# Renumbered expert rows, a combine tile from TensorE, and head outputs stored by halves

## The chip, the core and the metric

The kernel runs on one core of a Trainium2 chip. A core has five engines with queues of their own: TensorE (matrix products, PE in the profile, with PEld for the loading of its weights), VectorE (DVE), ScalarE (ACT), GpSimd (POOL) and SyncE (SP), which only issues transfers here. Sixteen DMA engines move data between the chip's memory (HBM, "DRAM" in the code) and the on-chip SBUF; TensorE writes to PSUM. The metric is the device time in microseconds of one execution. Before the change it was 1862.59 us, the median of three runs (1858.78 to 1864.37).

## What is computed

One transformer block over 2048 tokens of width 256: attention with 16 heads of 128 whose weights come as codes and scales, then a mixture of 8 experts with inner width 176, of which each token uses two. A layernorm stands before and after each half.

```python
x = x + _layernorm(attn(_layernorm(x)))        # 16 heads, softmax over 2048 keys
x = x + _layernorm(ffn(_layernorm(x)))
# ffn:
router_logits = jnp.einsum('bsh,he->bse', x, Wr)
probs = jax.nn.softmax(router_logits.astype(jnp.float32), axis=-1)
topk_w, topk_idx = jax.lax.top_k(probs, K)                       # K = 2
topk_w = topk_w / jnp.sum(topk_w, axis=-1, keepdims=True)
combine = jnp.einsum('bsk,bske->bse', topk_w, one_hot(topk_idx, E))
g = jnp.einsum('bsh,ehi->besi', x, Wg)
u = jnp.einsum('bsh,ehi->besi', x, Wu)
y = jnp.einsum('besi,eih->besh', jax.nn.silu(g) * u, Wd)
out = jnp.einsum('bse,besh->bsh', combine, y)
```

The kernel computes all experts for all tokens and multiplies the inner activations of each expert by the token's combine weight, which is zero for six experts of eight. So the experts become one dense layer with EI = 8×176 = 1408 inner rows, in 11 chunks of 128 (NCH).

## The kernel before

**Attention.** A loop runs over 256 steps, 16 heads times 16 tiles of 128 query rows. In each step TensorE makes a tile's scores against 2048 keys (L484 to L488), VectorE their maximum (L489), ScalarE the exponentials (L500). The probabilities are split into two float16 parts, `ph` (ScalarE, L514) and `pl` (VectorE, L529), and each part is transposed by a DMA that SP issues (L517, L535) into `pth` and `ptl`, 512 KB each. TensorE then multiplies them by the values (`pv_part`, L552), 13 half-steps behind. The finished output of a head for a block of 512 tokens is split into a high and a low half in float16 (`o`, GpSimd, L567 and L568) and stored to DRAM in `ot_d[b]`, laid out [128, head, 2, 512], by a DMA that GpSimd issues (L569).

**Hand-over.** From the last head on (`late`, L700), other loads share SP's queue with the transposes: output-projection weights, the gate weights `gu_raw` for `gw`, and the head outputs `oi` (`load_oi`, L681: four heads, both parts, 256 of the 512 tokens; 32 such loads in all). `op_mm` (L802) projects them (64 matmuls for half a block) and VectorE takes the layernorm statistics. The lines L1068 to L1138 write this stretch out by hand, in the order in which each engine gets its instructions. There the weights `wg`, `wu` and `wd` are split into two float32r parts by `split_piece` (L655): a copy on ScalarE and a subtraction on GpSimd. The stages of `wu` and of `wd` share two buffers (tag "raw"), so a piece of `wd` (`load_d`, L1109) is loaded when GpSimd has finished with a piece of `wu`.

**Experts.** A loop over q = 0 to 45 (L1170) runs the chunks of four token blocks: `gate_up(b, c)` makes gate and up products of chunk c (12 matmuls, `gup`), ScalarE the sigmoid (L989), VectorE three products (L990, L991, L994), ScalarE and GpSimd the split `hh` (L982, L983); `down` for the chunk two places back follows on TensorE (12 matmuls, `dps`). Between the chunks the tables FIRST, PREP and PREP2 (L1140 to L1167) place the projection, layernorm, transposes and routing of later blocks. Three PSUM tiles ("s") serve the gate products and the running sum of `down`.

**The combine weight.** `router_c` (L919) makes a [token, expert] weight on VectorE, `router_d` (L934) transposes it on TensorE to [8, 512], and SP stores it to `ct_d[b]` in DRAM. A chunk's 128 rows are consecutive inner rows, so they belong to one, two or three experts; `load_cu` (L945) therefore loads for each chunk, two chunks ahead, a tile `cu` of 128 rows in one or two pieces, each repeating one expert's row of `ct_d`. L991 multiplies it in place with the up product.

Tokens lie in tiles as row `c*512 + t*128 + p` for block c, sub-tile t and partition p (L271, L727, L1067).

What orders the work is the order of the instructions in each engine's queue: all engines and SP take their instructions in the order written.

Of the kernel before, what the change touches and what calls it, by code (L numbers as in the profile page):

```python
# [25 lines left out]
E = 8  # L26
# [11 lines left out]
def sandwich(  # L38
# [27 lines left out]
    ot_d = [dram.tile([128, NH, 2, 512], HP, name=f"ot_d{b}") for b in range(4)]  # L66
    ct_d = [dram.tile([E, 512], F32, name=f"ct_d{b}") for b in range(4)]
# [202 lines left out]
    with tc.tile_pool(name="start", bufs=4) as st:  # L270
        xv = x.rearrange("b (c t p) d -> p (b c) t d", p=128, t=4)  # L271
# [268 lines left out]

    PV_ORDER = [(c, i) for c in range(16) for i in (0, 1)]
    PV_ORDER += [(c, 2) for c in range(16)]

    def pv_part(h, b, e):
# [11 lines left out]
        if e == 7:  # L556
            if (h, b) == (NH - 1, 3):
                o = kqv.tile([128, 2, 512], HP, name="o_last", tag="v", bufs=8)
                nc.scalar.activation(o[:, 0, :], ps, AF.Copy, scale=1.0 / PS)
                nc.vector.scalar_tensor_tensor(  # L560
                    o[:, 1, :], ps, 1.0 / PS, o[:, 0, :], ALU.mult, ALU.subtract
                )
            else:
                o = soft.tile([128, 2, 512], HP, name="o", bufs=1)
                t32 = soft.tile([128, 512], F32, name="t32")
                nc.scalar.activation(t32, ps, AF.Copy, scale=1.0 / PS)
                nc.gpsimd.tensor_copy(o[:, 0, :], t32)  # L567
                nc.gpsimd.tensor_tensor(o[:, 1, :], t32, o[:, 0, :], ALU.subtract)  # L568
            nc.gpsimd.dma_start(out=ot_d[b][:, h], in_=o)  # L569
# [101 lines left out]
    def split_gu(dst, i, stg, on_pool):  # L671
        kc, eh = divmod(i, 2)
        cs = slice(4 * I * eh, 4 * I * eh + 4 * I)
        split_piece(
            (dst[:, 0, kc, cs], dst[:, 1, kc, cs]),
            stg.rearrange("p e i -> p (e i)"), on_pool,
        )
# [3 lines left out]
    def load_oi(b, half, j, tag="kT"):  # L681
# [4 lines left out]
            out=oi, in_=ot_d[b][:, 4 * j : 4 * j + 4, :, bass.ts(half, 256)]  # L686
# [13 lines left out]
    def late(t):  # L700
# [9 lines left out]
        if t == 9:  # L710
            proj_ctx.close()
            rp = ctx.enter_context(tc.tile_pool(name="gw", bufs=1, side="right"))
            gw = rp.tile([128, 2, 2, EI], F32R)
# [13 lines left out]
    XV = x.rearrange("b (c t p) d -> p (b c) t d", p=128, t=4)  # L727
# [191 lines left out]
    def router_c(b):  # L919
# [11 lines left out]
        nc.vector.tensor_tensor(cw[:, 0], cw[:, 0], cw[:, 1], ALU.add)  # L931
        CW[b] = cw

    def router_d(b):  # L934
        cw = CW.pop(b)
        pc = psA.tile([E, 512], F32, name="pct", tag="pj")
        for t in range(4):
            nc.tensor.transpose(pc[:, bass.ts(t, 128)], cw[:, 0, t, :], ident)
        ct = small.tile([E, 512], F32, name="cT", bufs=1)
        nc.scalar.copy(ct, pc)  # L940
        nc.sync.dma_start(out=ct_d[b], in_=ct)
# [3 lines left out]
    def load_cu(b, c):  # L945
# [183 lines left out]
    for c in range(2):  # L1129
        load_cu(0, c)  # L1130
# [39 lines left out]
    for q in range(4 * NCH + 2):  # L1170
# [21 lines left out]
        if (b, c) == (1, 3):  # L1192
            load_oi(3, 1, 3)
# [39 lines left out]
```

## Time and profile before

The profile is of one execution of 1862.14 us, whose span from first to last instruction is 1860.3 us; the mean granted TensorE clock was 0.987 of full speed.

| | us | share of span | instructions |
|---|---|---|---|
| TensorE, matmuls | 1789.9 | 96% | 8890 |
| TensorE, weight loads | 937.8 | 50% | 8890 |
| VectorE | 1627.9 | 88% | 2267 |
| ScalarE | 1365.3 | 73% | 1730 |
| GpSimd | 941.2 | 51% | 929 |

| transfer | number | KB each | us from issue to landing (median) |
|---|---|---|---|
| `oi` from `ot_d` (SP) | 32 | 512 | 6.7 |
| `o` to `ot_d` (GpSimd) | 63, and one `o_last` | 256 | 4.0 |
| transposes `pth`, `ptl` (SP) | 256 each | 512 | 5.1, 5.5 |
| `cu` from `ct_d` (SP) | 72 pieces | 32 to 256 | 2.3 to 4.4 |
| x at the start (SP) | 4 | 512 | 4.7 |
| x for the residual (SP) | 4 | 512 | 6.5 |

How to read it: busy times are averages over stages with different limits. The attention fills the first 1540 us or so, the hand-over the next 100, and the expert loop the rest up to 1855. A matmul's busy time is modelled and overlaps its neighbours', so a full TensorE is recognised by the absence of idle time before its instructions rather than by the share. A line of the order-of-time view gives the start, the duration, the engine with the line of the code and the operation, what is written and read, and how many such instructions are merged into the line; the bracket has the idle time of the engine before it and what ended it. In that bracket, and in the view of waits, "<-" points to the releaser. DMA share is the mean busy share of the 16 DMA engines, where overlapping packets can give more than 1.

### The profile page before, as it was taken

The page shows a single profiled execution, that of the slowest core. Times are in us where ns is not written, and L with a number is a line of the kernel's source. Part 1 is how long each engine was busy: PE and PEld are TensorE (multiplying, and loading weights), DVE is VectorE, ACT ScalarE, POOL GpSimd, SP SyncE. Part 2 cuts the span into 40 slices and gives each one's busy share as a digit, 9 for nine tenths or more (in the row PEclk, how much of TensorE's full clock was granted, in tenths as well). Part 3 has the DMA queues.
Part 4 walks back from the last instruction along what each step waited for, and adds up shares of the span by engine and source line. Part 5 has one row for each costly group of instructions (what it writes and reads, how often), then busy time and mean ns, then how long its engine had stood idle before and what let it go on. Part 6 is the DMA issues. An engine that isn't in the chain of part 4 may idle for free. (4 is left out here: it accounts for less than half of the span.)

```text
span 1860.3 us, 25554 instructions
## 1 busy us (share of the span) xinstructions
PE 1789.9 (96%) x8890; PEld 937.8 (50%) x8890; DVE 1627.9 (88%) x2267; ACT 1365.3 (73%) x1730; POOL 941.2 (51%) x929
## 2 busy tenths in 40 slices
PE   6899999999999999999999999999999988899997
PEld 4344444444444444444444444444444434588886
DVE  7999999999999999999999899999999975558566
ACT  5788888888888888888888888888888765222232
POOL 3365566556655565556555655565445432323232
PEclk9999999999999999999999999999999999999999
DMA  2999999999999999999999999999999999972121
GB/s 84 175 201 200 198 203 201 198 195 204 202 190 199 203 200 192 204 200 200 194 198 199 185 197 197 201 198 195 190 196 201 215 215 237 247 199 69 52 75 51
DMA packets 1132529, 342.31 MB, mean 184 GB/s; under 512 B 1071232, under 2 KB 1119568, under 8 KB 1132400
## 3 DMA queue, kind: packets, MB, share of 16 engines
q1 hardware_dynamic: 1119712, 309.74, 90.3%
q0 software_dynamic: 10544, 29.40, 5.7%
q10 hardware_dynamic: 2144, 1.54, 0.3%
q8 instruction: 70, 1.15, 0.2%
q14 instruction: 59, 0.48, 0.1%
HBM read 53.22 MB, written 18.94 MB: 39 GB/s over the span
## 5 line engine op out<-in xcount | busy, mean ns | idle before, releaser
L529 DVE SCALAR_TENSOR_TENSOR pl<-p,m,ph 128x1024 f16<-128x1024 f32 x512 | 723.4, 1413 | 32.6 <-DMA ptl<-pl 27.9
L500 ACT ACTIVATE p<-s,m,ssc 128x1024 f32<-128x1024 f32 x512 | 612.2, 1200 | 186.2 <-DVE m L493 173.5
L489 DVE TENSOR_REDUCE m<-s 128x1 f32<-128x1024 f32 x512 | 622.2, 1215 | 24.9 <-PE s L488 23.2
L514 ACT ACTIVATE ph<-p,m 128x2048 f16<-128x2048 f32 x256 | 512.9, 2003 | 67.5 <-ACT t L235 20.3
L552 PE MATMUL pv<-pth,v 128*128 128x512 f16 x2048 | 508.1, 381 | 9.7 <-POOL v L268 4.7
L552 PEld LDWEIGHTS <-v 128*128 128x128 f16 x3072 | 301.7, 98 | 378.9 <-POOL v L268 7.8
L484 PE MATMUL s<-kT,qT 128*128 128x512 f16 x1024 | 389.9, 381 | 17.4 <-ACT p L500 16.3
L485 PE MATMUL s<-kT,qT 128*128 128x512 f16 x1024 | 390.0, 381 | 0.0
L488 PE MATMUL s<-kT,qT 128*128 128x512 f16 x1024 | 306.2, 381 | 0.0
L552 PE MATMUL pv<-ptl,v 128*128 128x512 f16 x1024 | 253.2, 380 | 0.0
L236 POOL CAST qT<-t 128x512 f16<-128x512 f32 x63 | 76.4, 1212 | 239.0 <-ACT t L235 239.0
L267 POOL CAST v<-t 128x256 f16<-128x256 f32 (+1 forms) x105 | 45.0, 429 | 266.5 <-ACT t L266 266.5
L485 PEld LDWEIGHTS <-qT 128*128 128x128 f16 x1024 | 100.4, 98 | 132.7 <-issue 28.4
L268 POOL TENSOR_TENSOR v<-t,v 128x256 f16<-128x256 f32 (+1 forms) x105 | 160.4, 1528 | 8.5
L488 PEld LDWEIGHTS <-qT 128*128 128x128 f16 x1024 | 100.5, 98 | 122.1 <-issue 2.2
L484 PEld LDWEIGHTS <-qT 128*128 128x128 f16 x1024 | 100.4, 98 | 110.4 <-issue 1.8
L983 POOL TENSOR_TENSOR hh<-sg,hh 128x512 fp32r<-128x512 f32 x42 | 54.6, 1299 | 146.2 <-ACT hh L982 109.3
L982 ACT CAST hh<-sg 128x512 fp32r<-128x512 f32 (+1 forms) x45 | 27.5, 611 | 120.0 <-DVE sg L994 119.9
L500 ACT ACTIVATION_READ_ACCUMULATOR p<-s,m,ssc 128x1 f32 x512 | 99.0, 193 | 0.0
L568 POOL TENSOR_TENSOR o<-t,o 128x512 f16<-128x512 f32 x63 | 96.2, 1527 | 5.2
L236 POOL CAST kT<-t 128x512 f16<-128x512 f32 x60 | 65.6, 1094 | 64.1 <-ACT t L235 64.1
L237 POOL TENSOR_TENSOR kT<-t,kT 128x512 f16<-128x512 f32 x60 | 88.0, 1467 | 5.1
(183 smaller groups left out, 1827.2 us busy)
## 6 DMA issues: line engine op xcount, KB each, us to landing
oi<-ot_d SPq DMA_DIRECT2D x32, 512.0 KB, 6.7
ot_d<-o POOLq DMA_DIRECT2D x63, 256.0 KB, 4.0
pth<-ph SPq DMA_TRANSPOSE x256, 5.1
ptl<-pl SPq DMA_TRANSPOSE x256, 5.5
cu<-ct_d SPq DMA_DIRECT2D x16, 256.0 KB, 3.9
xt<-in_L_attn_x SPq DMA_DIRECT2D x4, 512.0 KB, 4.7
x<-in_L_attn_x SPq DMA_DIRECT2D x4, 512.0 KB, 6.5
st_s<-in_L_attn_wv_scales POOLq DMA_DIRECT2D x28, 64.0 KB, 4.3
```

Of the source, the lines that this page charges most:

```text
L236: nc.gpsimd.tensor_copy(t[:, 0, :], t32)
L237: nc.gpsimd.tensor_tensor(t[:, 1, :], t32, t[:, 0, :], ALU.subtract)
L268: nc.gpsimd.tensor_tensor(v[:, 1, sl, :], t32, v[:, 0, sl, :], ALU.subtract)
L484: nc.tensor.matmul(s[:, j, :], q[:, 0, qc], k[:, 0, :], start=True, stop=False)
L485: nc.tensor.matmul(s[:, j, :], q[:, 0, qc], k[:, 1, :], start=False, stop=False)
L488: nc.tensor.matmul(s[:, j, :], q[:, 1, qc], k[:, 0, :], start=False, stop=True)
L489: nc.vector.tensor_reduce(m[:, half : half + 1], s, AX.XY, ALU.max)
L500: nc.scalar.activation(p[:, bass.ts(i, 1024)], s, AF.Exp, bias=m[:, 2:3], scale=ssc[:, 0:1], accum_out=m[:, 3 + i : 4 + i],)
L514: nc.scalar.activation(ph, p, AF.Copy, scale=m[:, 6:7])
L529: nc.vector.scalar_tensor_tensor(pl[:, cs], p[:, cs], m[:, 6:7], ph[:, cs], ALU.mult, ALU.subtract)
L552: nc.tensor.matmul(ps, V[(h // 2, c // 4)][:, i % 2, c % 4, dc], d[:, :, c, :], start=(n == 0), stop=(n == 47),)
L568: nc.gpsimd.tensor_tensor(o[:, 1, :], t32, o[:, 0, :], ALU.subtract)
```

## The change

Four edits go together.

- The inner rows are renumbered: chunk c holds rows r*11 + c, r = 0 to 15, of every expert, so partition e*16 + r of every chunk belongs to expert e. `split_gu` writes `gw` and `uw` in this order, reading its stage with a step of 11 elements; `wd` is loaded as "(p c) d", one run of rows to a partition.
- One combine tile then serves all chunks of a block. `router_c` ends with an add that also repeats each expert's weight 16 times (`cx`, 128x512), `router_d` transposes it with four transposes of [128, 128] and copies the result to `CU[b]` on ScalarE. `ct_d`, its store and all `cu` loads are gone. `gate_up` writes the product to a tile `cg` of its own. `router_c(0)` moves behind the issue of the first piece of `wd`, `router_d(0)` uses a PSUM tile of the tag "s", and the loads of the residual tiles x1(2) and x1(3) move from before the expert loop to chunk (0, 2) and chunk (1, 3).
- `ot_d` is laid out [128, 2, head, 2, 256]: a head's output is stored as two halves of 256 tokens, and each `oi` load reads one run for each partition (4 KB) instead of eight (512 B). A store writes two runs of 1 KB for each partition instead of one of 2 KB.
- Tokens lie in tiles as row `c*512 + p*4 + t`, four consecutive tokens to a partition, for x, its second load and the output.

```diff
-    ot_d = [dram.tile([128, NH, 2, 512], HP, name=f"ot_d{b}") for b in range(4)]
-    ct_d = [dram.tile([E, 512], F32, name=f"ct_d{b}") for b in range(4)]
+    ot_d = [dram.tile([128, 2, NH, 2, 256], HP, name=f"ot_d{b}") for b in range(4)]
...
-        xv = x.rearrange("b (c t p) d -> p (b c) t d", p=128, t=4)
+        xv = x.rearrange("b (c p t) d -> p (b c) t d", p=128, t=4)
...
-                o = soft.tile([128, 2, 512], HP, name="o", bufs=1)
+                o = soft.tile([128, 2, 2, 256], HP, name="o", bufs=1)
...
-                nc.gpsimd.tensor_copy(o[:, 0, :], t32)
-                nc.gpsimd.tensor_tensor(o[:, 1, :], t32, o[:, 0, :], ALU.subtract)
-            nc.gpsimd.dma_start(out=ot_d[b][:, h], in_=o)
+                nc.gpsimd.tensor_copy(o[:, :, 0, :], halves(t32))
+                nc.gpsimd.tensor_tensor(
+                    o[:, :, 1, :], halves(t32), o[:, :, 0, :], ALU.subtract
+                )
+            nc.gpsimd.dma_start(
+                out=ot_d[b][:, :, h].rearrange("p f l q -> p f (l q)"),
+                in_=o.rearrange("p f l q -> p f (l q)"),
+            )
...
-        cs = slice(4 * I * eh, 4 * I * eh + 4 * I)
+        cs = slice(64 * eh, 64 * eh + 64)
         split_piece(
-            (dst[:, 0, kc, cs], dst[:, 1, kc, cs]),
-            stg.rearrange("p e i -> p (e i)"), on_pool,
+            (dst[:, 0, kc, :, cs], dst[:, 1, kc, :, cs]),
+            stg.rearrange("p e i -> p (e i)").rearrange("p (r c) -> p c r", c=NCH), on_pool,
         )
...
-            out=oi, in_=ot_d[b][:, 4 * j : 4 * j + 4, :, bass.ts(half, 256)]
+            out=oi.rearrange("p h l q -> p (h l q)"),
+            in_=ot_d[b][:, half, 4 * j : 4 * j + 4].rearrange("p h l q -> p (h l q)"),
...
-            gw = rp.tile([128, 2, 2, EI], F32R)
+            gw = rp.tile([128, 2, 2, NCH, 128], F32R)
...
-        nc.vector.tensor_tensor(cw[:, 0], cw[:, 0], cw[:, 1], ALU.add)
-        CW[b] = cw
-
-    def router_d(b):
-        cw = CW.pop(b)
-        pc = psA.tile([E, 512], F32, name="pct", tag="pj")
+        cx = tl.tile([128, 4, 8, 16], F32, name="cx", tag="sg", bufs=3)
+        sx = [128, 4, 8, 16]
+        nc.vector.tensor_tensor(
+            cx, cw[:, 0].unsqueeze(3).to_broadcast(sx), cw[:, 1].unsqueeze(3).to_broadcast(sx),
+            ALU.add,
+        )
+        CW[b] = cx
+
+    def router_d(b, tag="pj"):
+        cx = CW.pop(b)
+        pc = aux_psum([128, 512], F32, "pct", tag)
         for t in range(4):
-            nc.tensor.transpose(pc[:, bass.ts(t, 128)], cw[:, 0, t, :], ident)
-        ct = small.tile([E, 512], F32, name="cT", bufs=1)
-        nc.scalar.copy(ct, pc)
-        nc.sync.dma_start(out=ct_d[b], in_=ct)
-
-    def load_cu(b, c):
...
+            nc.tensor.transpose(
+                pc[:, bass.ts(t, 128)], cx[:, t].rearrange("p e r -> p (e r)"), ident
+            )
+        CU[b] = tl.tile([128, 512], F32, name="cu", bufs=2)
+        nc.scalar.copy(CU[b], pc)
...
-                        ps[:, i], w[:, wl, kc, cs], xT[a][:, kc, :],
+                        ps[:, i], w[:, wl, kc, c], xT[a][:, kc, :],
...
-        cu = CU.pop((b, c))
+        cu = CU[b]
+        cg = tl.tile([128, 512], F32, name="cg", bufs=2)
...
-            nc.vector.tensor_tensor(cu[:, fs], cu[:, fs], ps[:, 1, fs], ALU.mult)
+            nc.vector.tensor_tensor(cg[:, fs], cu[:, fs], ps[:, 1, fs], ALU.mult)
...
-    router_c(0)
     for i in range(2, 4):
         split_gu(uw, i, ust[i], True)
...
-    dsrc = wd.rearrange("e i d -> (e i) d").rearrange("(c p) d -> p c d", p=128)
+    dsrc = wd.rearrange("e i d -> (e i) d").rearrange("(p c) d -> p c d", c=NCH)
...
     d0 = load_d(0)
+    router_c(0)
     op_mm(1, 0, (3,), "s")
-    router_d(0)
-    for c in range(2):
-        load_cu(0, c)
+    router_d(0, "s")
     d1 = load_d(4)
-    load_x1(2)
-    load_x1(3)
...
-        2: [lambda: ln_c(1), lambda: split_d(*d2)],
+        2: [lambda: ln_c(1), lambda: split_d(*d2), lambda: load_x1(2)],
...
-        if q + 2 < 4 * NCH:
-            load_cu(*divmod(q + 2, NCH))
...
             load_oi(3, 1, 3)
+            load_x1(3)
```

The same pattern "(c p t)" is used for the second load of x and for the output, the same halves for `o_last`, and the same shape for `uw`.

## The prediction

> **What bounds the kernel now.** I read first the slices of the span, then TensorE's own idle times with their releasers, then the order of time around those idle times, and last the rates that the DMA engines reach.
>
> ```profile
> PE   6899999999999999999999999999999988899997
> DMA  2999999999999999999999999999999999972121
> ```
>
> ```profile
> PE s L484 <- ACT p L500: 7.8, 10, 2.1
> PE pv L552 <- POOL v L268: 4.7, 7, 0.8
> ```
>
> The first two lines are busy tenths in 40 slices of 46.5 us; the other two are TensorE's longest waits (total, times, longest) from 100 to 1500 us. TensorE sets the attention's pace: it waits some 14 us in 1400. After about 1663 us (slices 36 to 39) it is full again; its waits between there and 1845 us are 0.3 us or less. Between lies the hand-over, about 1522 to 1647 us (slices 33 to 35), where it is not full and DMA is. A time saved elsewhere than there, at the start (30 us of short chains) or behind the last matmul buys nothing. This is its order of time (start, duration, engine, line, operation; in brackets the idle time before it):
>
> ```profile
> 1608.49 3.30 POOL L658 TENSOR_TENSOR uw<-gu_raw,uw 128x704 fp32r<-128x704 f32 x2 [3.55 <-ACT uw L656]
> 1610.19 0.37 SPq L1112 DMA_DIRECT2D draw<-in_L_ffn_Wd  x1
> 1610.61 0.46 SPq L941 DMA_DIRECT2D ct_d<-cT  x1
> 1614.49 1.31 SPq L952 DMA_DIRECT2D cu<-ct_d  x3
> 1615.91 0.40 SPq L1112 DMA_DIRECT2D draw<-in_L_ffn_Wd  x1
> ...
> 1621.32 1.05 ACT L656 CAST dw<-draw 128x1024 fp32r<-128x1024 f32 x1 [4.66 <-DMA draw<-in_L_ffn_Wd]
> 1622.28 0.59 ACT L989 ACTIVATE sg<-gup 128x512 f32<-128x512 f32 x1
> ...
> 1626.10 0.60 PE L1008 MATMUL dps<-dw,hh 128*128 128x256 f32 x2 [1.87 <-ACT hh L982]
> 1627.59 2.50 PE L1008 MATMUL dps<-dw,hh 128*128 128x256 f32 x10 [0.89 <-POOL hh L983]
> 1631.17 2.93 PE L969 MATMUL gup<-xT,gw 128*128 128x512 f32 x6 [1.08 <-DVE cu L991]
> ...
> 1646.01 0.69 DVE L991 TENSOR_TENSOR cu<-cu,gup 128x512 f32<-128x512 f32 x1 [11.55 <-DMA cu<-ct_d]
> ...
> 1646.76 1.65 PE L969 MATMUL gup<-xT,gw 128*128 128x512 f32 x6 [1.65 <-DVE cu L991]
> ```
>
> Read it from SP's queue (SPq). The small store of `ct_d` goes out at 1610.61; the loads of `cu` must wait until it lands, 1614.49; and the second piece of Wd stands behind them, to 1615.91, though its buffer was free when GpSimd ended its split at 1611.79. ScalarE is in order: its copy of that piece at 1621.32 holds up the first sigmoid (1622.28), although the first gate matmuls were done at 1617.3. Hence the three idle times of TensorE, 3.84 us, and the half clock behind them: gate_up(0,3) takes from 1631.17 to 1636.6, 5.5 us, where later chunks take 2.75. Then `cu` of chunk 2, queued behind eight loads of `oi` of which the eighth waited for a buffer (issue of `cu` at 1640.31), stops VectorE for 11.55 us and TensorE for the last 1.65.
>
> **The change, part by part.**
>
> *Combine tile on TensorE.* Gone are 72 `cu` loads (the page's issues: 16+7×8), 4 `ct_d` stores and the round trip. TensorE's four transposes stay four: their moving side, 128 columns, is the same (272 ns with an 8-wide weight, 281 ns for the existing `trp` with a 128-wide one). ScalarE's copy goes from 8x512 to 128x512, 572 to about 590 ns. VectorE's closing add goes from 128x32 (192 ns) to 128x512; the nearest row is `sg<-sg,cu`, 711 ns, so +0.52 us a block. For blocks 1 to 3 the full TensorE hides it. For block 0 TensorE already waits 0.42 us at that add: **+0.5 us**. `cg` instead of multiplying in place is the same 0.68 us; the `sg` buffer that `cx` borrows for about one chunk leaves two, and one `sg` lives 4.7 us (1676.0 to 1680.7) against a chunk period of 4.2: enough. If TensorE were not full, the 54 `cu` loads of blocks 1 to 3 would be worth something; now they are worth nothing.
>
> *Order on SP's queue.* Nothing stands between the two Wd pieces except their buffers, which GpSimd's `uw` splits free. Those splits now read rows 44 bytes apart (every 11th float). The trace shows no such read: its packed row is 1.67 us for 704. The Trainium skill, "GPSIMD Engine Reference", section "Performance pitfalls for Q7 kernels", speaks against the change: reads with a byte step over 8 cost about half as much again, so 2.5 us. No run here shows it. By the row the second piece is issued at 1611.8 (4.1 us sooner), by the rule at 1611.8+2×0.83 = 1613.5 (2.4 us sooner). No row is near, so I take the rule. Then: landing +5.4 us (as both pieces did) 1618.9, copy 1.05, sigmoid 0.59, VectorE from 1620.5 (was 1622.9). GpSimd's split of the piece (2.39) and the pow (up to 1.5) end at about 1623.9 (was 1626.3), and ln_b1, chunk 1 and gate_up(0,3) follow **2.4 us** sooner, at 1628.8.
>
> *The clock.* TensorE would end down(0,0) at about 1626.1 and idle some 2.5 us. In this trace an idle time of 2.36 us (1570.9 to 1573.3) left the clock at 1.00, one of 2.90 us was followed by 0.81, and 1.87+0.89 us with two matmuls between by 0.72. The Trainium skill, "TensorE: Matmul & The Clock Gate", section "Part 1: The HAM clock gate", puts the fall after a wholly idle window of about 3.4 us, so by it no idle time here would do it; the 2.90 us row differs from it, and the measurement decides: 2.5 us is at the edge. By the rule, and by the 2.36 us row which is nearest, gate_up(0,3) and down(0,1) take 4.2 us instead of 6.8: **2.6 us** gained; by the 2.90 us row nothing. I take the gain.
>
> *The cu wait.* op_pass(2,0) then runs 1633.0 to 1640.0 and gate_up(0,4) starts at once: **1.65 us**. Its `oi` (four loads and the last Wd piece, 2.5 MB, from about 1620) lands by 1629, since the loads of x1(2) and x1(3) no longer stand ahead. Those two move to places after 1634; they are needed some ten chunks later. Sum: 2.4+2.6+1.65−0.5 = **6.1 us**.
>
> *oi in runs of 4 KB instead of 512 B.* Compare the DMA rates (last column) where almost only 1 KB runs moved (x at the start) and where mostly 512 B runs of `oi` did:
>
> ```profile
> core 0: us, PE busy (x) PEld busy (x) DVE busy (x) ACT busy (x) POOL busy (x), PEclk, DMA share, GB/s
> 4.00:6.00 2.00, 0.00 (x0) 0.00 (x0) 1.28 (x4) 0.00 (x0) 0.00 (x0) 1.00 1.11 351
> 1622.00:1632.00 10.00, 6.16 (x24) 4.75 (x23) 8.06 (x12) 2.11 (x5) 5.08 (x3) 0.72 1.12 297
> ```
>
> 524 KB take 1.49 us at 351 GB/s and 1.77 at 297: 0.28 us a load. Eight such loads pass before the last transpose of `ptl` lands at 1585.9, in a stretch where VectorE waits for those transposes (18.7 us in 8 waits), and the layernorm that leads to the first transposes of block 0 starts on that landing: 8×0.28 = **2.2 us**. From below 0, if the transposes' own 256-byte pieces set the pace; from above 4.5 us, if a load costs the 2.05 us that six issues took each from 1619.57 to 1631.89.
>
> *The rest.* The `o` store is cut into 256 runs of 1 KB: its issue on GpSimd goes towards the 742 ns of `woc`'s 256 runs, from 586; +0.16 us, hidden by a GpSimd that is half idle. The halved `o` costs the same (steps of 2 and 4 bytes); its 1.15 or 2.0 us lengths stand already in the trace. The `gw` splits read with the same stride, on ScalarE too: 0.77 us, between that and, for want of a row, double, 4×0.77 = 3.1 us at worst; ScalarE idles 5.65 us there before one of its 2.00 us copies (1534.46), so I take 0 and keep 3.1. x and out in 4 KB and 2 KB runs: the start waits for the scales (6.60 us) as much as for x; 0, within ±1. The slower `uw` splits 0 and 1 push the issue of oi(1,1) from 1600.2 to about 1601.9; its landing near 1607 still precedes 1608.9.
>
> Sum: −2.2−6.1 = −8.3 us against the profiled execution's 1862.14 (span 1860.3), **1853.8**; that execution lay 0.45 us under the median, so about **1854**.
>
> **Rivals.**
> - *The drain gains more* (1846): 4.5 us from `oi`, unstrided prices (4.1 instead of 2.4), and a 2.90 us idle time that shrinks and keeps its clock (24 `pv` took 7.04 us where 5.2 is usual: 1.9). Together 6.1+1.7+4.5+1.9 = 14.2, so 1848; with 1 to 2 from the start, 1846. For it: the DMA share of 1.1 there. Against: the transposes dominate it.
> - *The clock still falls and TensorE only changes what it waits for* (1858): without the 2.6 and with half of the `oi` gain, 3.5+1.1 = 4.6 us. For it: the row of 2.90 us, and VectorE's ln_b1 between chunks 0 and 1, which is late next.
> - *The strided splits become the bound, slower* (1868): GpSimd's `uw` splits free the Wd buffers and the stage of the next loads. At 4.2 us a split instead of 1.67 the second Wd piece goes out at 1616.9 and oi(1,1) at about 1605, and all is eaten up: that is the deciding point. At 5.7 us the piece is 4 us later than now and op_mm(1,1) waits some 4.5 for its loads; less the 2.2 and 1.65, about 5 us slower. For it: two such splits run back to back exactly there; against: the rule asks 1.5 times, not 3.4.
> - *It doesn't do what it says*: the loads vanish but the next wait on the same queue ends no sooner, 1862. Against: nothing but a buffer holds the second piece.
>
> **How the numbers follow.** Forecast 0.47 (1850 to 1857), more gain 0.21, clock 0.20, slower 0.07, no effect 0.05. Eight in ten: the lower end is 1846, the upper 1861, which holds the clock case and leaves out the slower one. A difference of 0.3% is 5.6 us, what a measurement of this kernel tells from none: faster needs 1857.0 or less. Faster 0.47+0.21+0.05 (from the clock case) = 0.73; slower 0.05; the rest, 0.22, within.
>
> **What would show it.** Right: no `cu` wait on VectorE; the second Wd issue within 4 us of the first; the first sigmoid within 3 us of the first gate matmuls; gate_up(0,4) some 8 us sooner, and all after it in equal steps. Wrong: `uw` splits over 4 us; the granted clock under 0.8 after down(0,0); `ptl`'s last landing not sooner than 1585; or a changed attention (100 to 1500 us).

## The result, and the profile after

The changed kernel takes **1848.88 us**, the median of five runs (1847.80 to 1851.07); the kernel before, run beside it, takes 1864.37 (1858.78 to 1864.96). The ratio is 0.9926, with a 95% interval of 0.9909 to 0.9942. A second set of six runs on another chip gave 1847.81 and 0.9926 (0.9901 to 0.9950). The profiled execution took 1847.86 us, its span is 1846.1 us: 14.2 us less than before, where 8.3 were forecast.

Four instants that both traces have cut the span into five pieces: TensorE's first projection matmul (op_mm(0,0)), the start of op_mm(1,1), the start of gate_up(0,4), and the end of VectorE's last addition. Below, the piece between the first and the second is called the first stretch, the next one the second stretch, and what follows the last addition the close.

| piece | before, us | after, us | change | forecast |
|---|---|---|---|---|
| start and attention, to op_mm(0,0) | 1562.0 | 1561.7 | -0.3 | 0 |
| first stretch, to op_mm(1,1) | 46.8 | 44.6 | -2.3 | -2.2 + 0.5 |
| second stretch, to gate_up(0,4) | 37.9 | 28.7 | -9.2 | -2.4 - 2.6 - 1.65 |
| to the end of the last addition | 207.6 | 208.0 | +0.4 | 0 |
| close | 6.0 | 3.2 | -2.8 | 0 |

A second trace of the changed kernel (the last experiment) has 1561.6, 45.1, 28.8, 208.0 and 3.2 us: half a us in one stretch of two single traces tells nothing.

In the page of the kernel after, the rows of busy tenths answer to the two shown of before. TensorE's row hardly tells the two kernels apart: it is full again from slice 36 on in both (slices of 46.2 us now), since tenths of a slice hide a gain of 14 us. The DMA row does: its last six slices, 972121 before, are 851000, since the loads of `cu` are gone.

```profile
PE   6899999999999999999999999999999888899998
...
DMA  2999999999999999999999999999999999851000
```

The order of time in the second stretch (start, duration, engine, line, operation; in brackets the idle time before it and its releaser) of the kernel after:

```profile
1605.99 4.02 POOL L666 TENSOR_TENSOR uw<-gu_raw,uw 128x704 fp32r<-128x704 f32 x2 [4.07 <-ACT uw L664]
...
1608.06 7.58 SPq L1112 DMA_DIRECT2D draw<-in_L_ffn_Wd  x3
...
1614.33 1.05 ACT L664 CAST dw<-draw 128x1024 fp32r<-128x1024 f32 x1 [1.51 <-DMA draw<-in_L_ffn_Wd]
...
1616.24 0.60 ACT L990 ACTIVATE sg<-gup 128x512 f32<-128x512 f32 x1 [0.86 <-PE gup L969]
...
1621.48 1.59 PE L1009 MATMUL dps<-dw,hh 128*128 128x256 f32 x12
...
1623.75 1.65 PE L969 MATMUL gup<-xT,gw 128*128 128x512 f32 x6 [0.68 <-DVE cg L992]
```

The three pieces of Wd now follow each other on SP's queue with nothing between them. ScalarE's copy of the second piece starts 8.0 us after op_mm(1,1) (at 1606.29) instead of 12.4, and the first sigmoid no longer waits behind it: its releaser is the gate product itself. Of TensorE's four idle times in this stretch (1.87, 0.89, 1.08 and 1.65 us) one of 0.68 us is left. The clock, in the last column but two of the view by windows, shows the rest; before, it was 0.72 from 1622 to 1640:

```profile
core 0: us, PE busy (x) PEld busy (x) DVE busy (x) ACT busy (x) POOL busy (x), PEclk, DMA share, GB/s
1622.00:1635.00 13.00, 12.32 (x98) 10.86 (x97) 10.73 (x23) 3.58 (x6) 6.78 (x5) 1.00 0.70 255
```

For the first stretch, TensorE's instructions that began after idle time, before:

```profile
1573.30 5.50 PE L814 MATMUL op_s<-wo,oi 128*128 128x256 bf16 x48 [2.36 <-DMA oi<-ot_d]
1581.69 7.04 PE L552 MATMUL pv<-pth,v 128*128 128x512 f16 x24 [2.90 <-DMA pth<-ph]
1590.84 3.73 PE L814 MATMUL op_s<-wo,oi 128*128 128x256 bf16 x32 [2.11 <-DMA oi<-ot_d]
...
1599.98 1.41 PE L876 MATMUL trp_s<-ident,at 128*128 128x128 f32 x7 [1.28 <-DVE at L841]
...
1608.45 0.60 PE L938 MATMUL pct<-ident,cw 128*8 128x128 f32 x4 [0.42 <-DVE cw L931]
```

and after:

```profile
1571.24 1.92 PE L823 MATMUL op_s<-wo,oi 128*128 128x256 bf16 x16 [0.59 <-DMA oi<-ot_d]
1573.34 3.67 PE L823 MATMUL op_s<-wo,oi 128*128 128x256 bf16 x32 [0.19 <-DMA oi<-ot_d]
1580.68 7.04 PE L554 MATMUL pv<-pth,v 128*128 128x512 f16 x24 [3.67 <-DMA pth<-ph]
1589.82 3.67 PE L823 MATMUL op_s<-wo,oi 128*128 128x256 bf16 x32 [2.10 <-DMA oi<-ot_d]
...
1605.80 0.66 PE L954 MATMUL pct_s<-ident,cx 128*128 128x128 f32 x4 [0.92 <-DVE cx L942]
```

Up to op_mm(1,0), the third line before and the fourth after, 0.7 us are gained (28.8 to 28.1): the first wait for `oi` shrinks by 1.6 us, and 0.8 comes back as a longer wait for `pth`, a transpose that SP issues. From there to the next 16 projection matmuls, at 1603.91 and 1600.77, 13.1 us become 10.95: the wait of 1.28 us for the layernorm (`at`) is gone, and its eight transposes run in one piece. The wait for `cx` then takes 0.5 back. Why the layernorm is no longer late stands in VectorE's first write of `at`, before:

```profile
1586.03 0.75 DVE L823 SCALAR_TENSOR_TENSOR at<-op_s,sig,crow 128x512 f32<-128x512 f32 x1 [15.78 <-DMA ptl<-pl]
```

and after:

```profile
1576.29 0.75 DVE L832 SCALAR_TENSOR_TENSOR at<-op_s,sig,crow 128x512 f32<-128x512 f32 x1 [6.96 <-DMA ot_d<-o]
```

The projection that it reads had ended long before in both. Before, it waited for the last transposing DMA of the attention, which reads `pl`; after, for the store of an earlier `o`. That is not a sooner landing of the same transfer, it is another transfer, and it comes 9.7 us sooner.

The close is the one piece about which the prediction said nothing. GpSimd's instructions at the program's end (operation, times, then min/median/max in ns, and starts), before:

```profile
L1229 POOLq DRAIN  x3: 46/102/7928, 1851.6 to 1860.1; - x3
```

and after:

```profile
L1225 POOLq DRAIN  x3: 46/102/1563, 1840.2 to 1845.8; - x3
```

A drain follows GpSimd's last computation. Before, it takes 7.93 us, to 1859.5, 5.2 us beyond VectorE's last addition, and the span ends 0.8 us later. After, it takes 1.56 us and is over before that addition.

### The profile page after: what moved, and what is told of

Same layout as the page of the kernel before. It is cut to its first block, busy times and chain, and to the rows that moved or that the text cites. A ratio compares the mean times of both kernels' runs of the same rounds, so it can differ in the third digit from the quotient of the medians.

```text
span 1846.1 us, 25409 instructions
## 1 busy us (share of the span) xinstructions
PE 1780.4 (96%) x8890; PEld 934.0 (51%) x8890; DVE 1626.4 (88%) x2267; ACT 1369.7 (74%) x1730; POOL 948.7 (51%) x929
## 5 line engine op out<-in xcount | busy, mean ns | idle before, releaser
L513 ACT ACTIVATE ph<-p,m 128x2048 f16<-128x2048 f32 x256 | 513.0, 2004 | 69.6 <-issue 22.3
L983 ACT CAST hh<-sg 128x512 fp32r<-128x512 f32 (+1 forms) x45 | 27.5, 611 | 107.1 <-DVE sg L995 107.0
```

The lines of the kernel that those rows point to most:

```text
L513: nc.scalar.activation(ph, p, AF.Copy, scale=m[:, 6:7])
```

## The experiments

The theories at the start were: **A**, each part works where the table has it (the queue of SP in the second stretch, the layout of `ot_d` and a tile's place in the first); **B**, one of these pieces belongs to another part. The spread matters for all that follows: the runs of one kernel differ by 3 to 16 us, and op_mm(0,0) starts between 1554.7 and 1563.9 us in the traces, so that pieces of the trace tell more than medians. There is one trace for each kernel, and a second for the kernel after.

**Tokens as before.** The kernel after with the old order of tokens, for x, its second load and the output.

```diff
-        xv = x.rearrange("b (c p t) d -> p (b c) t d", p=128, t=4)
+        xv = x.rearrange("b (c t p) d -> p (b c) t d", p=128, t=4)
```

> The changed kernel with the tokens laid out as before (sub-tile t, then partition), all else as changed. Measures: the first stretch (TensorE's first op_mm matmul to op_mm(1,1)) was 46.8 us before and 44.6 after; the second (op_mm(1,1) to gate_up(0,4)) 37.9 and 28.7; the close (end of VectorE's last add to the end of the span) 6.0 and 3.2. Theory A, four tokens to a partition are worth only the start: 0.3 us there, both stretches as after (44.6 and 28.7, each within 1), the close 3 to 4, time 1848 to 1850. Theory B, the 2.8 us of the close come from the longer runs of the output: the close back to about 6, time 1851 to 1852.

Measured: 1848.95 us (ratio 0.9932, 0.9909 to 0.9956), close 3.3, first stretch 45.2, second 28.6. The token order is worth nothing that can be measured, and the shorter close is not its doing.

**The old layout of ot_d.** The kernel after with `ot_d`, `o` and the loads of `oi` as before.

```diff
-    ot_d = [dram.tile([128, 2, NH, 2, 256], HP, name=f"ot_d{b}") for b in range(4)]
+    ot_d = [dram.tile([128, NH, 2, 512], HP, name=f"ot_d{b}") for b in range(4)]
...
-            in_=ot_d[b][:, half, 4 * j : 4 * j + 4].rearrange("p h l q -> p (h l q)"),
+            in_=ot_d[b][:, 4 * j : 4 * j + 4, :, bass.ts(half, 256)]
```

> The changed kernel with the head outputs stored and loaded as before (oi in runs of 512 bytes). Theory A, as predicted, the long runs relieve the DMA engines in the hand-over: the first stretch 1 to 3 us longer than 44.6, the second up to 2 us longer since op_mm(2,0) needs four oi, time +2 us or more (1851). Theory B, the hand-over's first stretch gained only by where the tile at lies: first stretch within 0.7 of 44.6, second within 0.7 of 28.7, time unchanged (1848 to 1850).

Measured: 1852.73 us (0.9953, 0.9939 to 0.9967), 3.8 more than the run above on the same chip. The first stretch is 45.4, 0.8 longer than in the kernel after and 0.3 longer than in its second trace, which is less than A asked. The close is 6.0, and GpSimd's drain stands there as before:

```profile
L1221 POOLq DRAIN  x3: 46/102/7930, 1843.0 to 1851.5; - x3
```

So A had the time right and its place wrong: 2.8 of the 3.8 us are in the close, and the other 1.0 is within the spread of the runs.

**One run of 1 KB.** To part the store's layout from the load's, `ot_d` gets 128 unused elements behind each 512. A store still writes 256 runs of 1 KB; a load of `oi` now reads four runs of 1 KB for each partition.

```diff
-    ot_d = [dram.tile([128, 2, NH, 2, 256], HP, name=f"ot_d{b}") for b in range(4)]
+    ot_d = [dram.tile([128, 2, NH, 640], HP, name=f"ot_d{b}") for b in range(4)]
...
+            in_=ot_d[b][:, half, 4 * j : 4 * j + 4, :512],
```

> The kernel after, but ot_d has 128 unused elements behind each 512, so that a load of oi reads four runs of 1 KB for each partition instead of one of 4 KB, while a store of o writes the same two runs of 1 KB. Theory A (the length of the runs that oi reads sets its landing, and the layout of the store sets the close behind the last add): the median landing of oi rises from 5.0 us to 5.3 to 6.0 (1 KB runs, between the 4 KB ones and the 512 B ones with 6.3 to 6.7), the first stretch (first op_mm matmul to op_mm(1,1)) from 44.6 us to 44.8 to 45.5, and the close stays at 3.2 us with GpSimd's last drain at 1.6 us; time 1849 to 1850. Theory B (the close follows the runs of the load): the close is 6.0 us, GpSimd's last drain 7.9 us, time 1851 to 1853.

Measured: 1848.92 us (0.9945, 0.9923 to 0.9967), close 3.2, drain 1.56 us, first stretch 44.7. The list of DMA issues (transfers, KB each, median us to landing) has

```profile
oi<-ot_d SPq DMA_DIRECT2D x32, 512.0 KB, 5.8
```

against 5.0 to 5.8 in the eight traces with 4 KB and 6.3 to 7.0 in the five with 512 B. A holds for the close: it follows the store. Between loads of 1 KB and of 4 KB no difference is resolved.

**Two stores of 1 KB runs.** The kernel after with the old layout again, but each `o` stored by two transfers of 128 runs of 1 KB (shown against the store of the old layout).

```diff
-            nc.gpsimd.dma_start(out=ot_d[b][:, h], in_=o)
+            for l in (0, 1):
+                nc.gpsimd.dma_start(out=ot_d[b][:, h, l], in_=o[:, l])
```

> The kernel after with the old layout of ot_d and the old loads of oi, but each store of o in two transfers of 128 runs of 1 KB instead of one of 128 runs of 2 KB. Theory A (the close behind the last add follows the number of runs that GpSimd's stores write, 256 a head output): GpSimd's last drain 1.6 us, close 3.2. Theory B (it follows the transfers' layout or number): drain 7.9 us and close 6.0, or a third value.

Measured (one execution): 1853.42 us, close 3.2; the drain has a third value:

```profile
L1222 POOLq DRAIN  x3: 46/102/3272, 1845.5 to 1851.1; - x3
```

The close of A comes, its drain does not quite: 3.27 us is short enough to end beside the output's transfers. Over all traces the drain is 7.93 us in the four kernels whose stores write 128 runs of 2 KB, 1.56 us in the eight that write 256 runs of 1 KB in one transfer, and 3.27 us here. That the store's form decides it is shown; what GpSimd drains, some 240 us after its last store, is open. The first stretch is 50.0 here, with a wait of 5.3 us for `oi`.

**The order on SP's queue alone.** The kernel before, with the second piece of Wd ahead of the `cu` loads and the two residual loads moved as in the change.

```diff
-    for c in range(2):
-        load_cu(0, c)
-    d1 = load_d(4)
-    load_x1(2)
-    load_x1(3)
+    d1 = load_d(4)
+    for c in range(2):
+        load_cu(0, c)
```

> The kernel before, with one thing of the change alone: on SP's queue the second piece of Wd goes ahead of the first cu loads, and the loads of x1(2) and x1(3) move to chunks (0,2) and (1,3); the cu loads stay. Theory A, the queue's order is most of the gain: second stretch 30 to 32 us instead of 37.9, with the wait for cu at gate_up(0,4) left (1 to 2 us), first stretch 46.8 within 1, time 1855 to 1858. Theory B, the cu loads themselves hold the stretch (their transfers or their places in the queue): second stretch 35 or more, time 1861 or more.

Measured: 1856.15 us (0.9967, 0.9957 to 0.9976), second stretch 33.0. TensorE and VectorE in the second stretch:

```profile
1623.09 2.35 DVE L841 TENSOR_SCALAR at<-at,mv,ln_r 128x256 f32<-128x256 f32 x4 [0.93 <-POOL ln_r L81]
...
1627.22 0.68 DVE L991 TENSOR_TENSOR cu<-cu,gup 128x512 f32<-128x512 f32 x1
...
1627.95 1.81 PE L969 MATMUL gup<-xT,gw 128*128 128x512 f32 x6 [1.92 <-DVE cu L991]
...
1629.56 2.76 PE L969 MATMUL gup<-xT,uw 128*128 128x512 f32 x6
...
1641.54 0.69 DVE L991 TENSOR_TENSOR cu<-cu,gup 128x512 f32<-128x512 f32 x1 [10.29 <-DMA cu<-ct_d]
...
1642.28 1.66 PE L969 MATMUL gup<-xT,gw 128*128 128x512 f32 x6 [1.30 <-DVE cu L991]
```

Order alone takes 4.9 of the 9.2 us. It leaves what only the tile removes: the wait for `cu` behind eight loads of `oi` (10.29 us on VectorE, 1.30 on TensorE). It also leaves an idle time of 1.92 us after which six matmuls take 2.76 us instead of 1.52, and that is no wait for a load of `cu`: VectorE's product at 1627.22 follows the layernorm of block 1 with no wait, and this layernorm starts 1.2 us later in relation to op_mm(1,1) than in the kernel after, since ScalarE gets the first piece of Wd 1.0 us later (6.5 against 5.5) and GpSimd's `ln_r` takes 1.49 us instead of 1.03. Whether the `cu` loads delay that piece is not shown. A's kind of split, a little further to the tile's side than A said (30 to 32).

**The residual loads back.** The kernel after with x1(2) and x1(3) loaded before the expert loop again.

```diff
     d1 = load_d(4)
+    load_x1(2)
+    load_x1(3)
     split_d(*d0)
```

> The kernel after with the loads of x1(2) and x1(3) back before the expert loop, between the second and the third piece of Wd. Theory A (with the cu loads gone the place of these two does not matter): the oi loads of op_pass(2,0) still land before 1628, the stretch from op_mm(1,1) to gate_up(0,4) stays at 28.4 to 29.0 us. Theory B (two loads of 512 KB ahead of oi delay op_pass(2,0)): that pass waits 1 to 3 us for oi, the stretch is 29.7 to 32 us.

Measured (one execution): second stretch 29.6, 1848.28 us. Neither theory: no instruction waits for `oi`, but ScalarE's copy of the second Wd piece starts 8.5 instead of 8.0 us after op_mm(1,1), the layernorm behind it 0.9 later (0.5 of it because GpSimd's `ln_r` takes 1.52 us instead of 1.03), and TensorE waits 1.60 us instead of 0.68 at gate_up(0,3). So the two loads cost nothing to those behind them. That they slow the piece ahead by sharing the DMA engines with it is possible but not shown: in the trace of the pad tile below, which lacks them there, the copy starts as late (8.4). The eight traces with the loads moved and these instructions in the same order have second stretches of 28.6 to 29.2 us, so the move is worth 0.4 to 1.0.

**A tile's place.** What had made `at` wait for another transfer? The change removes `cT`, 2 KB in the pool `small`, so tiles allocated behind it lie elsewhere. A tile of that size is put back into the kernel after, with one small copy to it.

```diff
         lg = small.tile([128, 4, 8], F32, name="lg", bufs=1)
+        if b == 0:
+            pad = small.tile([E, 512], F32, name="pad", bufs=1)
+            nc.vector.tensor_copy(pad[:8, :32], ps[:8, 0:4].rearrange("p t e -> p (t e)"))
```

> The changed kernel with a 2 KB tile added to the pool that lost one of that size (cT), and a small copy of 32 columns into it, so that the tiles behind it lie where they lay before. Theory A, the layernorm of block 0 started 9.7 us sooner because the tile at no longer lies over pl and no longer waits for the transpose that reads it: with the pad VectorE's first write of at waits for ptl again and starts at 1583 or later (after: 1576.3), the first stretch is 1 to 2.5 us longer than 44.6. Theory B, it started sooner for another reason: start within 2 us of 1576.3, first stretch within 0.7 of 44.6.

Measured: 1850.82 us (0.9938, 0.9919 to 0.9956). VectorE's order of time:

```profile
1577.94 0.75 DVE L832 SCALAR_TENSOR_TENSOR at<-op_s,sig,crow 128x512 f32<-128x512 f32 x1 [15.48 <-DMA ptl<-pl]
```

and TensorE's:

```profile
1582.41 5.33 PE L823 MATMUL op_s<-wo,oi 128*128 128x256 bf16 x32 [2.06 <-DMA oi<-ot_d]
...
1592.59 1.41 PE L885 MATMUL trp_s<-ident,at 128*128 128x128 f32 x7 [0.85 <-DVE at L850]
```

The attention ended 7 us sooner in this execution, so the instants of the expectation do not fit, but the distances do: `at` starts 23.3 us after op_mm(0,0), as before (24.0) and unlike after (14.6), and its old releaser is back. The first stretch is 47.5, 2.9 longer, all of it from op_mm(1,0) on: the piece of 10.95 us takes 14.1. Of the 3.2, 0.85 is the wait for the transposes of the layernorm, some 0.6 their being cut in two, and 1.7 the slow clock under op_mm(1,0) (5.33 us for 32 matmuls that take 3.67 after). The slow clock need not be the tile's doing: after, nearly the same idle time, 2.10 us, was not followed by one. So the place is worth 1.5 us here, or more, since at full clock TensorE would have come to these transposes sooner and waited longer.

**The same in the kernel before.** `cT` moves to a buffer of another pool; no instruction is added.

```diff
-        ct = small.tile([E, 512], F32, name="cT", bufs=1)
+        ct = tl.tile([E, 512], F32, name="cT", tag="sg", bufs=3)
```

> The kernel before, with one edit: the tile cT (8x512) takes a buffer of the tag sg in the pool tl instead of a place of its own in the pool small. No instruction is added or removed. Theory A (the layernorm of block 0 starts late only because its tile lies where the last pl lay, so that it must wait for the last transposing DMA; without cT's 2 KB the tiles behind it move): VectorE's first write of at comes 8 to 16 us after the first op_mm matmul (24.0 us in the kernel before, 14.5 after), and the stretch from the first op_mm matmul to op_mm(1,1) falls from 46.8 us to 44 to 45.5; the time to 1859 to 1861. Theory B (at comes sooner because oi lands sooner): at stays at 22 to 25 us, the stretch at 46 to 47.5, the time within 1 us of 1862.

Measured: 1861.79 us, ratio 1.0001 (0.9988 to 1.0015): no difference is resolved, and the interval reaches from 2.2 us less to 2.8 more. VectorE's order of time has the releaser that A expected:

```profile
1571.76 0.75 DVE L823 SCALAR_TENSOR_TENSOR at<-op_s,sig,crow 128x512 f32<-128x512 f32 x1 [1.45 <-DMA ot_d<-o]
```

but TensorE's has

```profile
1592.66 6.20 PE L814 MATMUL op_s<-wo,oi 128*128 128x256 bf16 x32 [5.50 <-DMA oi<-ot_d]
```

The layernorm starts 14.6 us sooner. But op_mm(1,0) starts 1.5 us later, after a wait of 5.50 us for `oi`, and runs at a lower clock (6.20 us instead of 3.73). The piece behind it takes 13.5 us; less the 2.5 of the clock that is 11.0, as after. The first stretch is 48.8. So A's mechanism is shown, and by this subtraction its 2 us are there, but in this trace the later `oi` and the clock take more: that the place alone buys time is not shown. Whether the sooner layernorm itself delays `oi` isn't told by one trace; the same wait of 5.3 to 5.5 us also came with the two stores, which has 512 B loads and an early `at` too, but not with the old layout of `ot_d`, which has both (2.2 us).

Taken together: from op_mm(0,0) to op_mm(1,0), the five traces with 512 B loads take 27.5 to 30.9 us, 29.3 in the mean; the nine with longer runs 25.6 to 28.7, 27.7 in the mean. The difference is some 1.5 us, with a spread as large in each group. And the piece behind it takes 10.95 to 11.01 us in all nine traces with an early `at` in which op_mm(1,0) ran at full clock, against 13.1 before. So the tile's place is shown as a cause of the first stretch's gain; that the longer runs are the other agrees with these means but is not clear of their spread.

**Packed reads.** The kernel after, but `gw` and `uw` split from packed columns.

```diff
-            stg.rearrange("p e i -> p (e i)").rearrange("p (r c) -> p c r", c=NCH), on_pool,
+            stg.rearrange("p e i -> p (e i)").rearrange("p (c r) -> p c r", c=NCH), on_pool,
```

> The kernel after, but the splits of gw and uw read their stage packed (64 consecutive columns for each chunk) and write where they wrote. This changes what is computed: gate and up rows then stand in another order than the rows of Wd. It prices the reads with a step of 44 bytes and nothing else. Theory A (the strided reads cost their engines but lie beside other work): the four gw copies on ScalarE fall from 1.43 us to 0.77, the splits on GpSimd from 2.05 to about 1.67; the second Wd piece goes out up to 0.8 us sooner, which shortens the stretch from op_mm(1,1) to gate_up(0,4), 28.7 us in the kernel after, by at most 0.7 us; the time stays within 1 us of 1848.9. Theory B (they hold up the exponentials, and with them TensorE): TensorE's long wait for an exponential near 1538 us, 5.2 us in the kernel after and 4.2 before, falls to 4.2 or less, and the time to 1846 to 1847.5.

The groups of instructions from 1500 to 1620 us (busy us, mean ns) of the kernel after:

```profile
L666 POOL TENSOR_TENSOR uw<-gu_raw,uw 128x704 fp32r<-128x704 f32 x4 | 8.2, 2066 | 4.9 <-ACT uw L664 4.9
L666 POOL TENSOR_TENSOR gw<-gu_raw,gw 128x704 fp32r<-128x704 f32 x4 | 8.2, 2046 | 18.4 <-ACT gw L664 18.4
L664 ACT CAST gw<-gu_raw 128x704 fp32r<-128x704 f32 x4 | 5.7, 1433 | 0.0
```

and with packed reads:

```profile
L666 POOL TENSOR_TENSOR gw<-gu_raw,gw 128x704 fp32r<-128x704 f32 x4 | 8.3, 2074 | 17.4 <-ACT gw L664 17.4
L666 POOL TENSOR_TENSOR uw<-gu_raw,uw 128x704 fp32r<-128x704 f32 x4 | 6.9, 1754 | 3.7 <-ACT uw L664 3.4 <-DMA gu_raw<-in_L_ffn_Wu 0.3
L664 ACT CAST gw<-gu_raw 128x704 fp32r<-128x704 f32 x4 | 3.1, 770 | 0.0
```

The stride costs ScalarE 86% (0.77 to 1.43 us) and GpSimd 18% on `uw` (1.75 to 2.07). GpSimd's `gw` splits, beside a busy VectorE, take 2.05 us with or without it. The first Wd piece goes out 0.8 us sooner in relation to op_mm(1,1), and the second stretch is 28.6, the same: the price lies beside TensorE's work. The long wait for an exponential is 4.96 us, so B's sign is not there, though the median is 1846.01 us (0.9931, 0.9912 to 0.9949), where B put it. The unchanged kernel after had 3.2 us of that wait in its second trace and runs from 1841 to 1851, so neither figure decides; a loss of a us or two in the attention is neither shown nor excluded.

**Hiding the wait for cx.** `router_d(0)` moves behind the first half of op_mm(1,1).

```diff
-    router_d(0, "s")
     d1 = load_d(4)
+    op_mm(1, 1, (0, 1), "s")
+    router_d(0, "s")
     split_d(*d0)
     split_d(*d1)
-    op_mm(1, 1, (0, 1, 2, 3), "s")
+    op_mm(1, 1, (2, 3), "s")
```

> The kernel after, with router_d(0) moved behind the first half of op_mm(1,1), so that TensorE has 3.5 us of matmuls before it needs cx. Theory A (TensorE's wait of 0.92 us for cx is pure loss there): the wait is gone, op_mm(1,1) starts 1.4 to 1.6 us sooner in relation to op_mm(1,0) (its four transposes now stand behind it), gate_up(0,0) starts 0.9 us sooner, and the stretch from the first op_mm matmul to gate_up(0,4), 73.2 us in the kernel after, is 72.1 to 72.5; time 1848. Theory B (something else is late next: ScalarE's copy of the combine tile now stands behind the first copy of Wd or the sigmoid, and the first cg product waits for it): gate_up(0,3) waits 1.5 us or more instead of 0.68, and nothing is gained, 73.0 or more.

Measured: 1848.28 us (0.9940, 0.9923 to 0.9958), and 73.9 us from op_mm(0,0) to gate_up(0,4). From op_mm(1,0), behind which the edit acts, it is 47.4 us instead of 45.1. VectorE's layernorm of block 1 and TensorE:

```profile
1617.36 2.35 DVE L850 TENSOR_SCALAR at<-at,mv,ln_r 128x256 f32<-128x256 f32 x4 [0.93 <-POOL ln_r L80]
...
1619.74 1.22 DVE L862 TENSOR_TENSOR x<-at,x 128x1024 f32<-128x1024 f32 x1
1620.88 0.68 DVE L991 TENSOR_TENSOR sg<-sg,gup 128x512 f32<-128x512 f32 x1
...
1622.22 1.98 PE L969 MATMUL gup<-xT,gw 128*128 128x512 f32 x6 [2.12 <-DVE cg L992]
...
1623.99 2.76 PE L969 MATMUL gup<-xT,uw 128*128 128x512 f32 x6
```

B's outcome: the wait for `cx` is gone, and gate_up(0,3) waits 2.12 us instead, with slow matmuls behind it. But it is not ScalarE's copy that is late: VectorE has the layernorm between the products of chunks 0 and 1, and waits 0.93 us for GpSimd ahead of it.

**The layernorm a chunk later as well.** On top of the last edit, ln_b1(1) and ln_b2(1) one chunk later, ln_c(1) at the head of chunk 3, and router_d(1) one chunk later.

```diff
-        0: [lambda: ln_b1(1)],
-        1: [lambda: ln_b2(1)],
-        2: [lambda: ln_c(1), lambda: split_d(*d2), lambda: load_x1(2)],
-        3: [lambda: op_pass(2, 0, "pv")],
+        1: [lambda: ln_b1(1)],
+        2: [lambda: ln_b2(1), lambda: split_d(*d2), lambda: load_x1(2)],
+        3: [lambda: ln_c(1), lambda: op_pass(2, 0, "pv")],
...
```

> The kernel after, with router_d(0) behind the first half of op_mm(1,1), ln_b1(1) and ln_b2(1) one chunk later and ln_c(1) ahead of op_pass(2,0) in chunk 3, and router_d(1) one chunk later. Theory A (in the last experiment the gain of 0.92 us was lost because VectorE's layernorm of block 1 stood between the products of chunks 0 and 1, so that gate_up(0,3) waited 2.1 us and ran at half the clock): with that layernorm one chunk later gate_up(0,3) waits 0.3 us or less at full clock, the stretch from the first op_mm matmul to gate_up(0,4) is 71.3 to 72.2 us instead of 73.2, the rest to the last add 207.5 to 207.7 instead of 207.95; time 1.3 to 2.2 us below the kernel after on the same chip. Theory B (VectorE is the bound of these chunks, its work is only moved): the wait comes back at gate_up(0,4) or at the transposes of block 1, 73 us or more to gate_up(0,4), and no gain.

```profile
1617.17 0.69 DVE L991 TENSOR_TENSOR sg<-sg,gup 128x512 f32<-128x512 f32 x1 [1.18 <-ACT sg L990]
1617.77 0.68 DVE L992 TENSOR_TENSOR cg<-cu,gup 128x512 f32<-128x512 f32 x1
...
1619.10 2.36 DVE L850 TENSOR_SCALAR at<-at,mv,ln_r 128x256 f32<-128x256 f32 x4
...
1619.50 1.55 PE L969 MATMUL gup<-xT,gw 128*128 128x512 f32 x6
```

This order of time shows the products ahead of the layernorm, and gate_up(0,3) at full clock without a wait. From op_mm(1,0) to gate_up(0,4) this trace has 43.3 us; the kernel after has 45.1 and 45.3 in its two. All 68.9 us from op_mm(0,0) are 4 to 5 us fewer, but the rest of that is before op_mm(1,0), where the waits for `oi` happened not to come. The wait of 0.38 us at router_d(1) went too, and 0.69 us appeared at block 2's transposes, so the last part stays at 207.9.

**The kernel after again**, on the same chip.

> The kernel after, unchanged, as the neighbour of the other runs on this chip. Both theories: 1847 to 1850 us; first op_mm matmul to gate_up(0,4) 73 to 74 us, from there to the end of the last add 207.95, close 3.2.

Measured: 1847.81 us (1841.05 to 1849.33), and 1848.63 (1843.49 to 1852.82; 0.9942, 0.9922 to 0.9963) for the version above. The 2 us saved in the trace of the hand-over do not show in the time, whose spread is larger. A version that beats the changed kernel is not shown.

## Why the prediction was right, and where not

The sign and the range were right (1846 to 1861), and the forecast of 1854 was 5 us too high. The value is that of the rival in which the drain gains more (1848, or 1846), but only one of its parts came: the Wd term gained more (4.8 us, against its 4.1), while its 4.5 us from `oi` and the 1.9 us of clock at the 24 `pv` did not come (these take 7.04 us in both traces). The close, which no one forecast, stands in their place. That the rival's value fits is luck.

- **The second Wd piece** (2.4 us forecast): from op_mm(1,1) to gate_up(0,3) the traces have 22.3 and 17.5 us, so 4.8. The mechanism holds, the term was mis-sized, twice. The rule of the Trainium skill ("GPSIMD Engine Reference", "Performance pitfalls for Q7 kernels") made a strided split 2.5 us as an estimate from the row of 1.67; it is 2.07, and the second issue comes 3.3 us sooner in relation to op_mm(1,1) rather than 2.4. And from issue to copy 5.4 us were put down as before; it took 4.3, so that the copy comes 4.4 us sooner. Fewer loads beside it and its own longer runs are the likely reasons, not shown apart. GpSimd's `ln_r`, 1.03 us instead of 1.48, gives most of the rest.
- **The clock and the cu wait** (2.6 and 1.65): from gate_up(0,3) to gate_up(0,4) 15.6 became 11.2 us, 4.4 against 4.25, with a granted clock of 1.00 instead of 0.72. The wait for `cu` is right in mechanism and size; with the order alone it stays. For the clock only the size is right. The prediction expected TensorE to idle 2.5 us there and took the gain because a row of 2.36 us had kept its clock. It idles 0.68 us, since the term above gained twice its forecast, so the question did not arise; idle times of 1.92 us (the order alone) and 2.12 us (`cx` hidden) at the same place were followed by half the clock. That the 2.6 us came is luck.
- **oi in longer runs** (2.2): the step that failed. It let the shorter loads bring the last landing of `ptl` forward by 2.2 us, and the layernorm of block 0 start on it as before. In relation to op_mm(0,0) that landing moved by 0.7 us (23.9 to 23.2). A sooner layernorm is indeed what shortened the stretch (2.1 us behind op_mm(1,0)), but it doesn't wait for that transpose any more, because removing `cT` moved later tiles; two experiments turn this wait on and off by a tile's place alone. What is left to the loads is 0.7 us in this trace, ahead of op_mm(1,0). That the sum came out near (2.8 without the cost of `cx`) is luck. In the kernel before, no gain from the place alone is resolved (ratio 1.0001).
- **cx** (+0.5): 0.42 to 0.92 us, right. For the later blocks the prediction had it hidden by a full TensorE; block 1 costs 0.38 us more. A wait moved behind other work did come back as another, so this cost is not simply one instruction's.
- **The close** (nothing forecast): -2.8 us. The prediction counted the store's issue (0.59 to 0.70 us, hidden, as it said) and never asked what GpSimd does at the program's end. The 6.0 us behind the last addition stood in the profile of before, and 5.2 of them under a drain of 7.93 us. No row could have told that a store's form sets it.
- **Token order, strided gw, o by halves on its engines** (0): the first was taken back and changed nothing; the second's cost shows on its engines and in no stretch after op_mm(0,0); of the attention's 1562 us, no difference is resolved.
- **The rivals.** The clock that still falls did not happen in the changed kernel, but its reason, the layernorm between chunks 0 and 1, was what came next: it is the 0.68 us left, and 2.12 us as soon as TensorE is sooner. The slower case would have needed splits of 4.2 us; they took 2.07.

## What to carry to other kernels

Compare two traces by pieces between instants that both have, from the first instruction to the last: a gain of 2.8 us sat behind the last computation, in a drain that no busy time shows. When a tile is removed, look again at the releasers of the first writes behind it, since the place of later tiles decides which old transfer they wait for; and price such a wait by what TensorE waits for next, not by how much sooner the tile is written. On a queue, count what stands between two pieces of the same load, for the consumer that is in order (here ScalarE's copy ahead of a sigmoid) hands the delay on.

## What the hardware showed unexpectedly

- GpSimd's drain at the end took 7.93, 3.27 or 1.56 us by the form of stores that had ended some 240 us before, the same within 0.01 us in every kernel of one form.
- A read of 4-byte elements 44 bytes apart cost ScalarE 86% (0.77 to 1.43 us for 128x704) and GpSimd 18% (1.75 to 2.07).
- The length of an idle time did not by itself tell the clock after it: 2.10 us (after) was followed by 32 matmuls in 3.67 us, 2.06 us (the pad tile) by the same 32 in 5.33, and 2.12 us (`cx` hidden) by six in 2.76 instead of 1.52. In each of the 14 traces the granted clock changes only at instants that lie whole multiples of 3.41 us apart, and what tells is how much of one stretch between two such instants is idle. In the view by windows (columns as above: TensorE's busy time behind the length of the stretch, the granted clock in the last column but two), the kernel after has

```profile
1584.95:1588.36 3.41, 2.77 (x13) 1.08 (x11) 2.25 (x11) 1.59 (x2) 1.09 (x2) 1.00 1.07 359
1588.36:1591.77 3.41, 1.95 (x18) 1.76 (x19) 2.20 (x2) 1.18 (x1) 3.41 (x2) 1.00 1.02 411
```

  and the one with the pad tile

```profile
1579.88:1583.29 3.41, 1.35 (x11) 0.80 (x9) 2.17 (x8) 2.60 (x2) 1.04 (x1) 1.00 1.01 397
1583.29:1586.70 3.41, 3.41 (x18) 2.35 (x16) 3.34 (x8) 0.00 (x0) 0.00 (x0) 0.50 0.49 197
```

  The 2.10 us are cut by such an instant into 0.64 and 1.46; the 2.06 us lie in one stretch, and the next runs at half the clock. In all traces together, from 60 to 1835 us, there are 7208 such stretches at full clock. By the records' modelled ends of matmuls, all 51 with more than 2.025 us of idle time were followed by half the clock, none with less than 1.81, and 3 of the 17 between. The prediction's two rows fit: its 2.36 us were cut into 0.82 and 1.55, its 2.90 us lay in one stretch. The rule that the Trainium skill gives ("TensorE: Matmul & The Clock Gate", "Part 1: The HAM clock gate"), the fall after an idle window of about 3.4 us, has the right length here but asks too much: only 7 of the 54 falls followed a stretch that was wholly idle.
